# Four re-orderings in a four-layer convolution and scan kernel: gathers, tail units, the switch to layer 3, and half of T2

## The chip, the cores and the metric

The kernel runs on one NeuronCore of a Trainium2 chip. The metric is the device time of one execution in microseconds (us). TensorE is called PE, VectorE DVE, ScalarE ACT, GpSimd POOL and SyncE SP.

## The reference

The input x is a float32 image of 1024 channels and 64 x 64 positions. Four layers follow one another, each with a group norm ahead of it (32 groups) and a residual sum:

```python
x = x + L0(gn(x))   # a layer norm, then a decaying cumulative sum over the channels
x = x + L1(gn(x))   # 1x1 convolution, 1024 -> 1024, and bias
x = x + L2(gn(x))   # see below
x = x + L3(gn(x))   # 1x1 convolution, 1024 -> 1024, and bias

# L2
xz = silu(in_proj_w @ x + in_proj_b)           # 3072 rows: x_ssm, res, gate
x_ssm, res, gate = split(xz, 3)
xf = silu(conv1d(x_ssm, width 3, per channel)) # over the 4096 tokens
dt, B, C = dbc_w @ xf + dbc_b                  # 2 heads, 8 states
perm = argsort(score of a Mobius map)          # an order of the tokens for each head
# in that order: h = exp(dt*A)*h + dt*B*x ; y = C.h + D*x ; then back to the old order
y = y * silu(gate) + res
out = silu(out_proj_w @ y + out_proj_b)
```

## The kernel before, in words

Work runs in this order, one stage behind the other on PE: layer 0 (to about 385 us), layer 1 (to 620), the first third of layer 2's in_proj with its convolution over tokens (to 1075), a short tail of that stage (to 1127), the scan (to 1662), gate and out_proj (to 2375), layer 3 (to the end).

Image tiles are 128 channels by 512 positions (FB = 512), in pairs of position blocks (NP = 4 pairs); KH = 4 channel tiles make half the channels. The 1024 x 1024 products are made with a fast matrix scheme (Strassen and Winograd). In layer 1 and for the thirds WX and WR of in_proj it has one level: `multiply` (matmul at L832) makes seven products for each half of the output, with the operands b21, b11, b22 and the differences t2, t3, t1, t4, which `b_sets` prepares (L780 to L809): t1 = b12 - b11, t2 = b22 - t1, t3 = t2 - b11, t4 = b21 - t2, with `comb` at L790. It is a generator, so a caller advances it a step at a time; t1 is made on DVE and in most calls t2, t3, t4 on POOL. One such product is eight matmuls of 128 x 512, handed out as two "units" of about four, and `next_units(upto)` gives one more unit while fewer than `upto` were given.

For the gate, out_proj and layer 3 the scheme has two levels: `two_steps` runs jobs (gate and out for each pair, then "last" for layer 3), each with 7 outer products P1 to P7 of 7 inner products of eight 128 x 256 matmuls (L1670). A job takes 49 slots; `plan` hangs every other step (normalise, differences, additions, silu, statistics, loads) on a slot, and the loop at L1680 walks through the slots in order and writes each slot's product and then its steps into the queues. Odd slots belong to the outer product one step behind (L1682). The last out job has ORDER_C and ends with P7 and P4; the first job of layer 3 has ORDER_D and begins with P1 and P5. A name such as P4P5 is outer P4, inner P5. `next_norm` (L1479) puts the group norm of layer 3 on slots of the last out job: `begin` loads an ACT table set that holds Ln and Exp (L1485) and starts, each `go_on` takes one step (the matmuls gn_pg at L198 and gn_pv at L207, with DVE's gn_d between, L201 to L203), and `end` finishes (gn_v at L215, Ln and Exp at L168 and L169, scale and bias at L171 to L218). `fill` (L1438) applies the norm on ACT to make b11. Outputs of the out job pass an ACT silu (L1602), a DVE addition (L1604) and DVE statistics (L1477).

The engines' queues for these stages are written out by hand: inside `manual_schedule` the order of the Python calls is the order on DVE, PE, POOL and ACT. The loads that SP issues wait for their buffers.

The tail (L1239) follows the last convolution outputs (`follow`, `follow_on`) with a unit of WR between, up to six units; then `finish(NP - 1)` makes the last tokens' rows: silu of `end` (L1141), end_pt (L1143), end_dbc (L1151), softplus with Exp and Ln (L1162 to L1174), and DMAs of the rows into tok_d (L1186, L1188).

The scan goes through 74 chunks (NK). For chunk k: `gather` (POOL, L1266) brings 128 rows of tok_d into a tile "g"; `step_sums` (ACT, ds, L1274), `turn_rows` (PE, pr, L1280 and L1281), `spread_decay` (DVE), `cross` (PE, pg, L1302), `weigh` (DVE, G, L1310 to L1315), `apply` (PE, py, L1319, and ACT's copy y, L1324), `scatter` (POOL, L1328) into y_d. WR's units fill PE in between; their first parts go from PSUM into tiles "rg" (`put2b`, L1011 to L1014), and later parts are added there (L1018). POOL also sums weights for the later stages (s, L461 to L481). The loop at L1342 and on gathers four chunks ahead; PE gets eleven units ahead of chunk 0.

Of the kernel before, what the change touches and what calls it, by code (L numbers as in the profile page):

```python
# [9 lines left out]
F32 = mybir.dt.float32  # L10
# [8 lines left out]
P = 128  # L19
# [71 lines left out]
def tile_net(ctx: ExitStack, tc: tile.TileContext, x, par_d, cst_d, w_d, w2_d, dbcw_d, out):  # L91
# [141 lines left out]
        nc.sync.dma_start(tok_d[HEADS * N :, :], rows)  # L233


    lines = [const.tile([HEADS * NT, 2, P], F32, name=f"lines{i}") for i in range(2)]
    turned_ = [const.tile([P, 2, HEADS * NT], F32, name=f"turned{i}") for i in range(2)]
    swap = [const.tile([P, 2, P // 2], F32, name=f"swap{i}") for i in range(2)]
    order_i = const.tile([HEADS * NT, P], I32, name="order_i")
    nc.gpsimd.iota(order_i, pattern=[[1, P]], base=0, channel_multiplier=P)  # L240

    def make_scores():
# [534 lines left out]
    def b_sets(B, make, first=False, eng=None):  # L777

        def plain(name, row, col, upto=KH):
            B.setdefault(name, [])  # L780
            for k in range(len(B[name]), upto):
                t = b_tile(name, k, B["name"])
                make(t, row * KH + k, col)
                B[name].append(t)

        def comb(name, one, two, ks, eng):
            if name not in B:
                B[name] = [b_tile(name, k, B["name"]) for k in range(KH)]
            for k in ks:
                eng.tensor_tensor(B[name][k], B[one][k], B[two][k], ALU.subtract)  # L790

        slow = nc.vector if first else eng or nc.gpsimd
        plain("b21", 1, 0)
        yield
        plain("b11", 0, 0)
        yield
        plain("b22", 1, 1)
        yield
        for upto in (2, KH):
            plain("t1", 0, 1, upto)  # L800
            comb("t1", "t1", "b11", range(upto - 2, upto), nc.vector)
            yield
        comb("t2", "b22", "t1", range(KH), slow)
        yield
        for name, one, two in (("t3", "t2", "b11"), ("t4", "b21", "t2")):
            for ks in ((0, 1), (2, 3)):
                comb(name, one, two, ks, eng or nc.gpsimd)
                yield
# [196 lines left out]

    rg_pool = tc.tile_pool(name="l2r", bufs=2)
    rg_pools = [rg_pool.__enter__()]
    part, silus = {}, []  # L1010

    def put2b(m, o, nb, ps):
        part[o, nb] = rg_pools[-1].tile([P, FB], F32, tag="rg", name=f"rg{o}_{nb}")
        nc.scalar.copy(part[o, nb], ps)  # L1014

    def add2b(m, o, nb, ps):
# [12 lines left out]
    with tc.tile_pool(name="l2a", bufs=2) as pa, tc.tile_pool(name="l2a2", bufs=1) as pa2, \  # L1029
# [161 lines left out]
        with tc.manual_schedule(engines={E_.DVE, E_.PE, E_.Pool, E_.Activation}):  # L1191
            nc.sync.dma_start(both[:, :, P:], dbcw_d)
            nc.gpsimd.tensor_copy(both[:, :, :P], ident.unsqueeze(1).to_broadcast([P, CT, P]))
            nc.gpsimd.memset(row, 0.0)
            ends, i, chain = iter(()), -1, None
            for half in run(EARLY + LATE, [WX], normed(norm2), put2a, add2a, before2,
                            last_eng=nc.vector, fine=True, tell=True, begun=begun):
                if len(norm2) < CT:
                    n = len(SECOND)
                    if chain is None:  # L1200
                        moments("gn2b", SECOND, range(2, 4), mv2)
                        chain = norm_steps("gn2b", mv2[:, 0, :n], mv2[:, 1, :n], n, finer=True)
                        turns = 0
                    turns += 1
                    if turns < 3:
                        next(chain), next(chain)
                    else:
                        columns(SECOND, finish_of(chain), norm2)
                if half:
                    if coming[0] == "take":  # L1210
                        sort_on(True, 0)
                    if due3:
                        turn(*due3.pop(0))
                elif half is False:
                    turned = bool(due3)
                    follow()
                    follow_on()
                if half is not None:
                    continue
                i += 1  # L1220
                if i > 14 and i % 14 == 4:
                    ends = finish(i // 14 - 1)
                next(ends, None)
                if coming[0] != "turn" or not turned:
                    sort_on(True, (0, 0, 0, 1, 3, 1, 0, 2, 0, 2, 3, 3, 0, 0)[i % 14])
            while coming[0] is not None:
                sort_on(True, 1)

            forget(EARLY)
            units = run([3, 2] + EARLY, [WR], normed(norm2), put2b, add2b, before2, fine=True, B=last_B[0])  # L1230
            total, first, given = NP * 2 * NG * 7, 11, 0

            def next_units(upto):
                nonlocal given
                if given < upto:
                    given += 1
                    next(units, None)

            while ready or due or due2 or due3:  # L1239
                follow()  # L1240
                next_units(6)
                follow_on()
                next_units(6)
                activate(len(silus))
            for _ in finish(NP - 1):
                pass

    with tc.tile_pool(name="l2r2", bufs=8) as prg, tc.tile_pool(name="l2g", bufs=5) as pgat, tc.tile_pool(name="l2b", bufs=2) as pb, tc.tile_pool(name="l2h", bufs=1) as ph, \
            tc.tile_pool(name="ps2b", bufs=1, space=PSUM) as psb:
        rg_pools.append(prg)
        G2 = [ph.tile([P, P], F32, name=f"G{i}") for i in range(2)]
        B2 = [(ph.tile([MW, P], F32, name=f"bts{i}"), ph.tile([MW, S, LC], F32, name=f"cd{i}"))
              for i in range(2)]
# [81 lines left out]
        with tc.manual_schedule(engines={E_.DVE, E_.PE, E_.Pool, E_.Activation}):  # L1339
            while given < first:  # L1340
                next_units(total)
            for k in range(4):  # L1342
                gather(k)
            step_sums(0)
            for k in range(-1, NK + 1):
                upto = first + (k + 2) * (total - first) // (NK + 2)
                turned = turn_rows(k + 1) if k + 1 < NK else None
                if k > 0:
                    weigh(k - 1, pgs.pop(k - 1))
                if turned is not None:  # L1350
                    spread_decay(k + 1, *turned)
                if k + 2 < NK:
                    step_sums(k + 2)
                next_units(upto)
                y = apply(k - 1) if k > 0 else None
                if 0 <= k < NK:
                    pgs[k] = cross(k)
                if k + 1 < NK:
                    nc.scalar.activation(decay_[k + 1], decay_[k + 1], AF.Exp)
                if y is not None:  # L1360
                    scatter(k - 1, y)
                if 3 < k + 4 < NK:
                    gather(k + 4)
                next_units(upto)
                if given // 2 % 14 != 12:
                    next(sums, None)
                if len(silus) > 3:
                    activate(4)
            while given < total:
                next_units(total)  # L1370
            next(units, None)
            while silus:
                activate(4, nc.gpsimd)
            for _ in sums:
                pass
# [25 lines left out]
    def two_steps(jobs, norm2):  # L1401
# [76 lines left out]

        def next_norm(s0):  # L1479

            for row, slot, after, last in ((0, 44, (3, 3, 4, 4), 4), (1, 56, (3, 3, 4, 4), 5)):
                steps = {}

                def begin(row=row, steps=steps):
# [13 lines left out]
        def plan(j):  # L1498
# [9 lines left out]

            if kind != "out":
                for name, row, col, slot, when in (  # L1510
                        (("b11", 0, 0, -7, -1), ("b12", 0, 1, -3, 2), ("b21", 1, 0, 3, 12), ("b22", 1, 1, 8, 14))
                        if order is ORDER_D else
                        (("b11", 0, 0, -25, -14), ("b12", 0, 1, -14, -3), ("b21", 1, 0, -10, -1), ("b22", 1, 1, 1, 8))):
                    on(slot, fetch, src_d, pair, row, col, (j, "x", name))
                    for k in range(KH):
                        on(when + (k // 2 if when in (-1, 12) and order is ORDER_D else k), fill, j, name, row, col, k)
                late = [(1, "t1", "b12", "b11"), (9, "t2", "b22", "t1"), (13, "t3", "t2", "b11"), (27, "t4", "b21", "t2")]
                ks = [range(KH)] * 4
                put_in = {2: 12}
                if order is ORDER_D:  # L1520
                    late = [(2, "t1", "b12", "b11"), (16, "t2", "b22", "t1"), (20, "t3", "t2", "b11"), (27, "t4", "b21", "t2")]
                    put_in = {0: -1, 1: 5, 2: 13, 3: 19, 4: 24}
            else:
                late = [(14, "t1", "b12", "b11"), (15, "t2", "b22", "t1"), (19, "t3", "t2", "b11"), (34, "t4", "b21", "t2")]
                ks = [(2, 3, 0, 1), (2, 3, 0, 1), range(KH), range(KH)]
# [151 lines left out]
        for j in range(len(jobs)):  # L1677
            plan(j)
        end = len(jobs) * JOB
        for slot in range(min(at), max(max(at), end + 6) + 1):  # L1680
            step, i = divmod(slot, 7)
            if i % 2 == 1:  # L1682
                step -= 1
            if 0 <= step < 7 * len(jobs):
# [111 lines left out]
```

## Time and profile before

| | |
|---|---|
| median of 3 runs | 2735.13 us (2734.6 to 2735.33) |
| profiled execution | 2736.82 us |
| its span | 2735.0 us |
| PE busy in the span | 2613.8 us |
| DVE, POOL, ACT busy | 1804.5, 1224.4, 1089.8 us |
| mean granted PE clock | 0.983 of full |

The span runs from the first to the last record of the profiled execution; 1.8 us of its time lie outside. A wait is written as the engine that waits, the tile and line it wants to work on, and the engine, tile and line that released it, followed by the total in us, how often, and the longest. In a timeline a line has the start in us, the duration, engine, line, operation, output and input; idle time ahead of it and its releaser stand in square brackets. DMA lines show the issue, not the landing. The granted clock comes in stretches[...].

### The profile page before, as it was taken

To read this page: it belongs to the slowest core of one execution; us is meant where nothing else is said; L and a number is where in the kernel's file an instruction comes from. 1 tells how busy PE (TensorE), PEld (TensorE's weight loads), DVE (VectorE), ACT (ScalarE), POOL (GpSimd) and SP (SyncE) were. 2 spreads that over 40 slices of the span, in tenths; PEclk is the share of its full clock that TensorE was granted. 3 is DMA by queue.
4 is the path that set the end of the run, shared out by engine and by line. 5 is a ranking of instruction groups with operands and counts; after the bars stand their busy time and mean duration, and the time that the engine had idled before them with its cause. 6 is when DMAs were issued, how large, how long until landed. Compare 5 with 4: busy or idle time off the path is not lost.

```text
span 2735.0 us, 30900 instructions
## 1 busy us (share of the span) xinstructions
PE 2613.8 (96%) x9594; PEld 1726.7 (63%) x9594; DVE 1804.5 (66%) x3793; ACT 1089.8 (40%) x1840; POOL 1224.4 (45%) x1103
## 2 busy tenths in 40 slices
PE   4778999999999999999999999999999999999999
PEld 3664444444555555544444447888888888788887
DVE  7996765555445565477777665567576676777777
ACT  4783110104655654475757554322233133221220
POOL 4154224421112002357475655556575565555544
PEclk9998999999999999999999999999999999999999
DMA  7345557645433434587767874879899898788896
GB/s 286 119 166 185 175 206 262 202 131 202 162 106 107 138 129 102 162 267 223 228 195 226 274 222 144 243 246 304 217 277 292 239 304 234 251 289 294 298 328 214
DMA packets 423448, 591.46 MB, mean 216 GB/s; under 512 B 149973, under 2 KB 211541, under 8 KB 420214
## 3 DMA queue, kind: packets, MB, share of 16 engines
q1 hardware_dynamic: 298934, 365.76, 41.9%
q10 hardware_dynamic: 91456, 136.33, 14.2%
q0 software_dynamic: 32896, 87.40, 12.5%
q8 instruction: 78, 1.28, 0.2%
q14 instruction: 84, 0.69, 0.1%
HBM read 432.02 MB, written 157.36 MB: 215 GB/s over the span
## 4 chain that ended last, share of the span: by engine, by line
PE 47%; DMA 4%; POOL 3%; issue 3%; DVE 2%; ACT 1%; SPq 0%; POOLq 0%; DVEq 0%; ACTq 0%
PE mm L832 8%; PE q_P6P L1670 5%; PE q_P5P L1670 5%; PE q_P7P L1670 5%; PE q_P2P L1670 5%; PE q_P4P L1670 5%; PE q_P3P L1670 5%; PE q_P1P L1670 5%; DMA y_d<-y,dst 2%; PE py L1319 1%; POOL s L461 1%; PE pg L1302 1%; POOL t L790 1%; DMA g<-tok_d,src 0%; PE pr L1280 0%
## 5 line engine op out<-in xcount | busy, mean ns | idle before, releaser
L832 PE MATMUL mm<-t,w 128*128 128x512 f32 x1536 | 685.2, 597 | 4.6 <-POOL t L790 4.0
L832 PE MATMUL mm<-b,w 128*128 128x512 f32 x1152 | 516.4, 599 | 4.0 <-ACT b L936 2.9
L832 PEld LDWEIGHTS mm<-t,w 128*128 128x128 f32 x1536 | 286.7, 191 | 332.0 <-issue 318.1
L832 PEld LDWEIGHTS mm<-b,w 128*128 128x128 f32 x1152 | 216.8, 192 | 255.1 <-issue 243.7
L1328 POOL DMA_INDIRECT y_d<-y,dst x74 | 73.7, 996 | 184.6 <-ACT y L1324 107.4
L1055 DVE SCALAR_TENSOR_TENSOR cvp<-xs,par,cvp 128x512 f32<-128x512 f32 x128 | 95.3, 754 | 77.9 <-ACT cvp L1052 75.7
L1639 ACT COPY qQ<-q_P5P 128x512 f32<-128x512 f32 x48 | 28.1, 585 | 290.4 <-PE q_P5P L1670 239.5
L1082 POOL TENSOR_TENSOR acc<-l2xt,acc 128x136 f32<-128x136 f32 x56 | 28.2, 504 | 236.9 <-ACT l2xt L1076 233.6
L461 POOL TENSOR_TENSOR s<-s 128x256 f32<-128x256 f32 (+3 forms) x120 | 130.2, 1092 | 7.9
L790 POOL TENSOR_TENSOR t<-b,t 128x512 f32<-128x512 f32 x72 | 92.9, 1318 | 72.2 <-DVE t L790 48.1
L1322 ACT COPY g<-py 8x512 f32<-8x512 f32 x146 | 83.8, 574 | 95.0 <-PE py L1319 92.0
L1106 DVE TENSOR_TENSOR xs<-mm,xs 128x512 f32<-128x512 f32 x64 | 41.8, 684 | 117.8 <-PE mm L832 117.8
L951 DVE SCALAR_TENSOR_TENSOR image<-mm,par,image 128x512 f32<-128x512 f32 x64 | 47.2, 747 | 104.4 <-PE mm L832 104.3
L1310 DVE TENSOR_TENSOR E<-E,pg 128x512 f32<-128x512 f32 x74 | 50.7, 685 | 76.0 <-PE pg L1302 66.2
L1074 PEld LDWEIGHTS l2pt<-both,cv 128*128 128x128 f32 x512 | 77.2, 191 | 35.6 <-issue 24.6
L1438 ACT ACTIVATE qb<-x_x_b,gn_bias,gn_r_r 128x512 f32<-128x512 f32 x64 | 48.9, 806 | 113.9 <-DVE qQ L1600 50.5
L1670 PE MATMUL q_P4P<-t_t,wq_P4P 128*128 128x256 f32 x384 | 93.9, 389 | 0.0
L936 ACT ACTIVATE b<-image,gnl_bias,gnl_r_r 128x512 f32<-128x512 f32 x48 | 37.2, 809 | 138.1 <-PE mm L832 111.5
L1670 PE MATMUL q_P5P<-t_t,wq_P5P 128*128 128x256 f32 x384 | 90.8, 379 | 0.0
L1670 PE MATMUL q_P1P<-t_b,wq_P1P 128*128 128x256 f32 x384 | 90.6, 379 | 0.1
L1670 PE MATMUL q_P6P<-t_t,wq_P6P 128*128 128x256 f32 x384 | 90.7, 379 | 0.0
L1670 PE MATMUL q_P7P<-t_t,wq_P7P 128*128 128x256 f32 x384 | 90.7, 379 | 0.0
(415 smaller groups left out, 5914.6 us busy)
## 6 DMA issues: line engine op xcount, KB each, us to landing
w<-s_d SPq DMA_DIRECT2D x96, 512.0 KB
w<-in_w_dram SPq DMA_DIRECT2D x72, 512.0 KB
x_x_b<-x_d ACTq DMA_DIRECT2D x28, 1024.0 KB
image<-x_d SPq DMA_DIRECT2D x12, 2048.0 KB
wq_P6P<-s_d SPq DMA_DIRECT2D x84, 256.0 KB
wq_P7P<-s_d SPq DMA_DIRECT2D x84, 256.0 KB
wq_P5P<-s_d SPq DMA_DIRECT2D x84, 256.0 KB
wq_P3P<-s_d SPq DMA_DIRECT2D x84, 256.0 KB
```

Of the source, the lines that this page charges most:

```text
L461: eng.tensor_tensor(out, a, b, ALU.subtract)
L790: eng.tensor_tensor(B[name][k], B[one][k], B[two][k], ALU.subtract)
L832: nc.tensor.matmul(to[o], w[:, k, o * P : (o + 1) * P], B[name][k], start=(fresh and k == 0), stop=(k == KH - 1), skip_group_check=True)
L951: nc.vector.scalar_tensor_tensor(part, ps, pcol(bias_name, o), part, ALU.add, ALU.add)
L1055: nc.vector.scalar_tensor_tensor(cv, xo[:, at + t : at + t + FB], pcol("dww", 3 * o + t), cv, ALU.mult, ALU.add)
L1074: nc.tensor.matmul(pt[:, q * NV : (q + 1) * NV], cv[:, (q0 + q) * P : (q0 + q + 1) * P], both[:, o, :], start=True, stop=True)
L1106: nc.vector.tensor_tensor(part, ps, part, ALU.add)
L1310: nc.vector.tensor_tensor(Ef, Ef, pg, ALU.mult)
L1322: nc.scalar.copy(rows[k + 1][h * LC : h * LC + S, :DH], py[h * LC : h * LC + S])
L1328: nc.gpsimd.indirect_dma_start(out=y_d[:, :], out_offset=bass.IndirectOffsetOnAxis(ap=dst_[:, k : k + 1], axis=0), in_=y[:, :], in_offset= ...
L1438: nc.scalar.activation(tile_of(j, name)[:, k], held[j, "x", name][:, k], AF.Identity, bias=bias, scale=scale)
L1670: nc.tensor.matmul(ps[:, o, :], w[:, k, o * P : (o + 1) * P], rhs[:, k, :], start=(new and o == 0 and k == 0), stop=(k == 1), skip_group_c ...
```

## The change

Four things are re-ordered; no arithmetic is added or dropped.

- Gathers: five are issued ahead of the loop and chunk k + 5's in step k; six tiles "g" in place of five. The tiles of the token sort (lines, turned, swap, order_i) move into a pool that is closed ahead of the scan.
- Tail: up to eight units in place of six, with four "rg" tiles in the first pool in place of two; then `put2b` goes round a ring of ten tiles, six of the new pool and four of the old.
- The switch to layer 3: the first six slots of its first job are walked through in another order (1, 3, 5, 0, 2, 4), so the last three odd products of P4 come in a row ahead of the first three of P1; the steps of the first norm sit one or two slots later, and so do the first fills, the fetch of b21 and the first inner differences.
- T2: the first two of the four subtractions of t2 are written right behind t1's last ones, in the step before.

```diff
@@ -233,10 +233,12 @@
         nc.sync.dma_start(tok_d[HEADS * N :, :], rows)
 
 
-    lines = [const.tile([HEADS * NT, 2, P], F32, name=f"lines{i}") for i in range(2)]
-    turned_ = [const.tile([P, 2, HEADS * NT], F32, name=f"turned{i}") for i in range(2)]
-    swap = [const.tile([P, 2, P // 2], F32, name=f"swap{i}") for i in range(2)]
-    order_i = const.tile([HEADS * NT, P], I32, name="order_i")
+    sort_pool = tc.tile_pool(name="sort", bufs=1, side="right")
+    sorts = sort_pool.__enter__()
+    lines = [sorts.tile([HEADS * NT, 2, P], F32, name=f"lines{i}") for i in range(2)]
+    turned_ = [sorts.tile([P, 2, HEADS * NT], F32, name=f"turned{i}") for i in range(2)]
+    swap = [sorts.tile([P, 2, P // 2], F32, name=f"swap{i}") for i in range(2)]
+    order_i = sorts.tile([HEADS * NT, P], I32, name="order_i")
     nc.gpsimd.iota(order_i, pattern=[[1, P]], base=0, channel_multiplier=P)
 
     def make_scores():
@@ -799,8 +801,10 @@
         for upto in (2, KH):
             plain("t1", 0, 1, upto)
             comb("t1", "t1", "b11", range(upto - 2, upto), nc.vector)
+            if upto == KH:
+                comb("t2", "b22", "t1", range(2), slow)
             yield
-        comb("t2", "b22", "t1", range(KH), slow)
+        comb("t2", "b22", "t1", range(2, KH), slow)
         yield
         for name, one, two in (("t3", "t2", "b11"), ("t4", "b21", "t2")):
             for ks in ((0, 1), (2, 3)):
@@ -1005,12 +1009,15 @@
 
 
 
-    rg_pool = tc.tile_pool(name="l2r", bufs=2)
+    rg_pool = tc.tile_pool(name="l2r", bufs=4)
     rg_pools = [rg_pool.__enter__()]
     part, silus = {}, []
 
     def put2b(m, o, nb, ps):
-        part[o, nb] = rg_pools[-1].tile([P, FB], F32, tag="rg", name=f"rg{o}_{nb}")
+
+        at = rg_pools.pop(0)
+        rg_pools.append(at)
+        part[o, nb] = at.tile([P, FB], F32, tag="rg", name=f"rg{o}_{nb}")
         nc.scalar.copy(part[o, nb], ps)
 
     def add2b(m, o, nb, ps):
@@ -1238,20 +1245,22 @@
 
             while ready or due or due2 or due3:
                 follow()
-                next_units(6)
+                next_units(8)
                 follow_on()
-                next_units(6)
+                next_units(8)
                 activate(len(silus))
             for _ in finish(NP - 1):
                 pass
 
-
-
-
-
-    with tc.tile_pool(name="l2r2", bufs=8) as prg, tc.tile_pool(name="l2g", bufs=5) as pgat, tc.tile_pool(name="l2b", bufs=2) as pb, tc.tile_pool(name="l2h", bufs=1) as ph, \
+    sort_pool.__exit__(None, None, None)
+
+
+
+
+
+    with tc.tile_pool(name="l2r2", bufs=6) as prg, tc.tile_pool(name="l2g", bufs=6) as pgat, tc.tile_pool(name="l2b", bufs=2) as pb, tc.tile_pool(name="l2h", bufs=1) as ph, \
             tc.tile_pool(name="ps2b", bufs=1, space=PSUM) as psb:
-        rg_pools.append(prg)
+        rg_pools[:] = [prg] * 6 + rg_pools * 4
         G2 = [ph.tile([P, P], F32, name=f"G{i}") for i in range(2)]
         B2 = [(ph.tile([MW, P], F32, name=f"bts{i}"), ph.tile([MW, S, LC], F32, name=f"cd{i}"))
               for i in range(2)]
@@ -1339,7 +1348,7 @@
         with tc.manual_schedule(engines={E_.DVE, E_.PE, E_.Pool, E_.Activation}):
             while given < first:
                 next_units(total)
-            for k in range(4):
+            for k in range(5):
                 gather(k)
             step_sums(0)
             for k in range(-1, NK + 1):
@@ -1359,8 +1368,8 @@
                     nc.scalar.activation(decay_[k + 1], decay_[k + 1], AF.Exp)
                 if y is not None:
                     scatter(k - 1, y)
-                if 3 < k + 4 < NK:
-                    gather(k + 4)
+                if 4 < k + 5 < NK:
+                    gather(k + 5)
                 next_units(upto)
                 if given // 2 % 14 != 12:
                     next(sums, None)
@@ -1478,7 +1487,7 @@
 
         def next_norm(s0):
 
-            for row, slot, after, last in ((0, 44, (3, 3, 4, 4), 4), (1, 56, (3, 3, 4, 4), 5)):
+            for row, slot, after, last in ((0, 44, (4, 4, 5, 5), 6), (1, 56, (3, 3, 4, 4), 5)):
                 steps = {}
 
                 def begin(row=row, steps=steps):
@@ -1508,18 +1517,18 @@
 
             if kind != "out":
                 for name, row, col, slot, when in (
-                        (("b11", 0, 0, -7, -1), ("b12", 0, 1, -3, 2), ("b21", 1, 0, 3, 12), ("b22", 1, 1, 8, 14))
+                        (("b11", 0, 0, -7, 1), ("b12", 0, 1, -3, 2), ("b21", 1, 0, 5, 12), ("b22", 1, 1, 8, 14))
                         if order is ORDER_D else
                         (("b11", 0, 0, -25, -14), ("b12", 0, 1, -14, -3), ("b21", 1, 0, -10, -1), ("b22", 1, 1, 1, 8))):
                     on(slot, fetch, src_d, pair, row, col, (j, "x", name))
                     for k in range(KH):
-                        on(when + (k // 2 if when in (-1, 12) and order is ORDER_D else k), fill, j, name, row, col, k)
+                        on(when + (k // 2 if when in (1, 12) and order is ORDER_D else k), fill, j, name, row, col, k)
                 late = [(1, "t1", "b12", "b11"), (9, "t2", "b22", "t1"), (13, "t3", "t2", "b11"), (27, "t4", "b21", "t2")]
                 ks = [range(KH)] * 4
                 put_in = {2: 12}
                 if order is ORDER_D:
                     late = [(2, "t1", "b12", "b11"), (16, "t2", "b22", "t1"), (20, "t3", "t2", "b11"), (27, "t4", "b21", "t2")]
-                    put_in = {0: -1, 1: 5, 2: 13, 3: 19, 4: 24}
+                    put_in = {0: 2, 1: 5, 2: 13, 3: 19, 4: 24}
             else:
                 late = [(14, "t1", "b12", "b11"), (15, "t2", "b22", "t1"), (19, "t3", "t2", "b11"), (34, "t4", "b21", "t2")]
                 ks = [(2, 3, 0, 1), (2, 3, 0, 1), range(KH), range(KH)]
@@ -1677,8 +1686,11 @@
         for j in range(len(jobs)):
             plan(j)
         end = len(jobs) * JOB
+
+        s3 = turning * JOB
+        instead = {s3 + i: s3 + p for i, p in enumerate((1, 3, 5, 0, 2, 4))}
         for slot in range(min(at), max(max(at), end + 6) + 1):
-            step, i = divmod(slot, 7)
+            step, i = divmod(instead.get(slot, slot), 7)
             if i % 2 == 1:
                 step -= 1
             if 0 <= step < 7 * len(jobs):
```

## The prediction, on record before the change was run

> **What bounds the kernel now.** I read busy shares first, then the list of waits of TensorE (PE), then busy time by stage, then the timeline at each wait that the change touches. The page and the list of waits say:
>
> ```profile
> span 2735.0 us, 30900 instructions
> PE 2613.8 (96%) x9594; PEld 1726.7 (63%) x9594; DVE 1804.5 (66%) x3793; ACT 1089.8 (40%) x1840; POOL 1224.4 (45%) x1103
> PE pr L1280 <- DMA g<-tok_d,src: 7.6, 5, 2.8
> PE q_P1P L1670 <- ACT qb L1438: 5.4, 3, 2.7
> PE l2pt L1074 <- ACT l2xt L1076: 4.1, 1, 4.1
> PE mm L832 <- POOL t L790: 4.0, 1, 4.0
> ```
>
> PE is the bound: 2735.0 - 2613.8 leaves 121 us idle, about 77 of it in the first 400 us, which the change doesn't touch. So an edit can win only a PE wait and the half-clock time after it. By stage (columns: busy time of PE, PEld, DVE, ACT, POOL, granted clock, DMA share, GB/s):
>
> ```profile
> 1080.00:1110.00 30.00, 25.88 (x89) 15.13 (x88) 9.71 (x21) 13.54 (x26) 2.36 (x5) 0.94 0.35 107
> 1110.00:1130.00 20.00, 20.00 (x66) 9.32 (x65) 4.53 (x21) 7.32 (x16) 6.97 (x12) 1.00 0.70 201
> 1550.00:1600.00 50.00, 42.94 (x106) 19.39 (x106) 28.30 (x63) 23.52 (x43) 27.05 (x29) 0.93 0.84 262
> 2360.00:2412.00 52.00, 43.49 (x173) 34.79 (x172) 35.84 (x71) 24.64 (x38) 16.41 (x13) 0.87 0.76 260
> ```
>
> Late in the scan 7.1 us are idle and (1 - 0.93) x 50 = 3.5 us go to the clock; at the start of layer 3 it is 8.5 idle and 0.13 x 52 = 6.8 of clock. The hand-over to the scan (1110 to 1130) loses nothing: remember that row.
>
> **What the Trainium skill says.** "TensorE: Matmul & The Clock Gate", Part 1, "What's actually happening": the clock halves after at least one idle window of about 3.4 us and comes back after a busy one. The trace agrees on the sizes: eight matmuls of 128x256 take 1.89 us, but 3.76 after the 3.00 us wait at 2368.44. An idle stretch of some 3 us or more thus costs about 1.7 us on top (half of one window). "ScalarE: Activation LUTs", "What ACT_TABLE_LOAD costs": 1283 ns and a drain of 1380 ns. The trace has 1.28 us and no drain behind it (the load at 2380.02 is followed by ACTIVATE at 2381.32), so I use 1.28. The same page, "Table sets", says Ln and Exp share one set that can be loaded once; before, one load at 2361.91 serves both. "DMA: Bandwidth & Descriptors", "Anatomy of one DMA", has about 2 us fixed plus bytes; the gathers here measure more, 4.2 us when the DMA queues are light (1122.36 to 1126.54) and 5.5 to 5.9 late in the scan, which I use.
>
> **Gathers five chunks ahead (L1342, L1362).** POOL late in the scan, with the scatter (L1328) ahead of each gather (L1266):
>
> ```profile
> 1577.45 1.00 POOL L1328 DMA_INDIRECT y_d<-y,dst  x1
> 1578.75 0.96 POOL L1266 DMA_INDIRECT g<-tok_d,src  x1 [0.30 <-issue]
> 1583.96 1.00 POOL L1328 DMA_INDIRECT y_d<-y,dst  x1 [4.25 <-DMA y_d<-y,dst]
> 1585.27 0.97 POOL L1266 DMA_INDIRECT g<-tok_d,src  x1 [0.30 <-issue]
> 1584.72 0.55 PE L1280 MATMUL pr<-cst,g 128*112 128x192 f32 x2 [2.58 <-DMA g<-tok_d,src]
> ```
>
> The gather issued at 1578.75 is chunk 65's, which PE wants 3.4 us later and gets after 5.9. The five waits are 0.59, 0.19, 2.81, 2.58 and 1.41 us. One chunk more of lead is worth a period, (1644.16 - 1127.15) / 73 = 7.1 us. Chunks 63 to 66 together owe 6.8 us, and 2 to 3.5 more once PE isn't slowed: chunk 66 would be wanted near 1583.3. Its gather now takes the place of 65's and lands near 1584.7, so 1.3 us may stay. Gain: 7.6 + 3.5 - 1.3, **10 us** (4 to 12.5: POOL may slip, or all goes). The fifth gather ahead of the loop costs POOL 1.3 us, hidden: PE waits for the first alone. The count of instructions stays. Six buffers for g let the gather run without waiting for an earlier chunk's readers. The ring of ten rg tiles: the copies into them wait for PE (ACT's rg for mm, 37.7 us in 22 waits), none of weight for a tile. 0 (-0.5 to +0.5). Moving the sort's tiles frees room and has no instruction of its own.
>
> **Eight units in the tail (next_units(8), four l2r tiles).** The built order has the whole t2 product (8 matmuls) and one of t3 ahead of end_pt (L1143), where before there were one of t2. Before:
>
> ```profile
> 1110.80 0.27 PE L1143 MATMUL end_pt<-cst,end 128*8 128x128 f32 x1
> 1112.43 1.28 ACT L1165 ACT_TABLE_LOAD   x1
> 1113.96 1.28 ACT L1172 ACT_TABLE_LOAD   x1
> ...
> 1122.36 1.08 POOL L1266 DMA_INDIRECT g<-tok_d,src  x1 [0.17 <-issue]
> 1126.54 0.35 ACT L1274 ACTIVATE ds<-cst,g 128x64 f32<-128x64 f32 x1 [2.04 <-DMA g<-tok_d,src]
> 1127.15 0.49 PE L1280 MATMUL pr<-cst,g 128*112 128x192 f32 x2
> ```
>
> This is one chain: end_pt, softplus with two table loads, the last rows to HBM, the memsets that wait for those rows to land, gather 0, pr0. It takes 15.7 us, and before 18 matmuls of 0.857 us = 15.4 us of PE work lie beside it, so PE waits for nothing. After: t2 from 1109.95, 8 x 0.857 to 1116.8; the two rg copies (L1014, 0.59 each) stand ahead of `end` on ACT, which in turn stands ahead of end_pt: 1116.85 + 0.59 + 0.21, end_pt near 1117.75 instead of 1110.80, 6.95 us later. pr0 stays behind the eleventh unit, and only 11 matmuls (9.4 us) are left beside the chain. Its end moves to 1126.55 + 6.95 = 1133.5, PE is done at 1127.2: 6.3 us idle, and 1.7 of clock: **+8 us** (0 if the rows get out earlier by a path that I don't see, 9.5 with two half-clock windows). The 4.1 us wait at 1087.62 keeps its order: ACT's l2xt copy stands behind the same rg copies. 0.
>
> **Last quarters in a row ahead of layer 3 (L1481, L1511, L1680).** Before:
>
> ```profile
> 2361.91 1.28 ACT L1485 ACT_TABLE_LOAD   x1
> 2368.44 0.59 PE L198 MATMUL gn_pg<-gn_mv,cst 128*128 128x4 f32 x2 [3.00 <-DVE gn_mv L181]
> 2372.45 0.43 PE L207 MATMUL gn_pv<-gn_d,cst 128*128 128x4 f32 x2
> 2375.61 3.78 PE L1670 MATMUL q_P1P<-qb,wq_P1P 128*128 128x256 f32 x8 [2.74 <-ACT qb L1438]
> ```
>
> Four P4 and three P1 products alternate and are done at 2390.08. In the new order P4P7, P4P5, P4P4, P4P3 come first, then P1P1, P1P2, P1P6: the four P4 products (4 x 1.73 = 6.9 us) are to cover the norm's chain, which needed 7.2 us from pg to P1P1. But the chain grows. On ACT two silus of Q (L1602) now stand around the norm's Ln and Exp, so the preload is lost and the built order has four more loads: silu, Ln's, Exp's, silu's again. On DVE, Q's add and statistics stand inside the norm. Step by step: mv ends 2368.4, pg follows; P4P7 is done at 2367.2, but P4P5 waits for DVE to empty its bank: 2370.2 to 2372.1; d after one more add (0.6) at 2372.4; pv 2372.5; P4P4, P4P3 to 2376.1. DVE: two adds for P4P5, Q's add and statistics (4 x 0.65), v at 2375.1. ACT: Ln 2375.4, load 1.28, Exp 2376.9, load 1.28, silu 0.7: 2378.9. DVE: Q's second add and statistics 2380.3, four small operations 2381.1. Two fills of 0.8: P1P1 near 2382. PE idles 2376.1 to 2382 and pays half a clock again; P1P1 3.5, P1P2 1.9 to 3.5, P1P6 1.8: all seven done 2389 to 2391, against 2390.08. **+0.5**. P4P3's result is on DVE ten us sooner, so of the three small waits behind (1.08, 0.68, 0.56) I take 1.0 as gone: **-0.5** in all. Bounds: -13 (all idle and clock of the switch) to +5 (half clock throughout and P5P1's inputs late). SP's weight loads follow the new order ten buffers ahead; b21's fetch moves two slots later and is used from slot 12 on: 0.
>
> **Half of T2 in another step (L803).** In layer 1 no POOL instruction lies between its old place and the new, so the 4.0 us wait for t (L790) stays: there t2 sits behind s (L470), which waits 27.4 us for its DMA. In the scan two t2 (2.5 us) move ahead of one scatter and gather, three times; the longer lead covers it. 0 (-6.4 with its clock, if the order helped, to +1).
>
> **Sum**, against the profiled execution (2736.82 us, span 2735.0 and 1.8 around it): -10 + 8 - 0.5 = -2.5, so 2734.3. That execution lies 1.7 us above the median of 2735.13: **2732.6**, rounded 2732.5. Its own range: gathers -12 to -7, tail +6 to +9.5, switch -3 to +4: 2727 to 2740.
>
> **The rivals.** (1) *The switch works as meant*: the loads hide, P1P1 finds its input as P4P3 ends; 10 of the 13 us go, to 2736.8 - 10 + 8 - 10 - 1.7 = 2723; with the tail covered too, 2715. For it: 6.9 us of products against a chain of 7.2. Against: four loads, and Q on DVE within the norm. (2) *The slow side: POOL paces the gathers*. At 1583.96 the scatter ahead of the gather waits 4.25 us for the scatter before it to land; when these chained scatters (6.5 us each, against a period of 7.1) and the sums set the pace, the extra lead is spent once and the waits return later in the scan. Then the gathers give 1 us and the rest stands: 2736.8 - 1 + 7.5 - 1.7 = 2741.6. It decides from a gather gain under 2 us. For it: 12 such waits, 41.2 us. Against: they stop after chunk 67, and the debt is about one period. (3) *The change doesn't do what it says*: T2's move leaves layer 1's order as it is; I have that in the forecast. If it did act, 2726.
>
> **Chances.** Forecast 0.43, rival 1 0.32, rival 2 0.22, rival 3's opposite 0.03. 0.2% is about what a measurement of this kernel can tell from no change: below 2729.7 or above 2740.6. Faster: rival 1 0.30, the forecast's low end 0.05, the last 0.02: 0.37. Slower: rival 2's 0.20 and 0.03 of the forecast: 0.23. Same 0.40. To leave out no more than 0.2: 2717 to 2744.
>
> **What would show it.** Gathers: the wait of pr for g (7.6 us) nearly gone, ACT's ds for g far below its 82.0 us. Tail: a new wait of 6 us at pr0 near 1127; without it that step is wrong. Switch: four more table loads near 2365 to 2380 and a wait of about 6 us at P1P1; if P1P1 follows P4P3 at once, rival 1 holds. T2: the 4.0 us wait at t remains. Waits for g after chunk 60 as before would mean rival 2.

## The result and the profile after

The changed kernel takes 2742.88 us in the median of 10 runs (2740.66 to 2744.64); the kernel before took 2735.23 us beside it. The ratio is 1.0027, with a 95% interval of 1.0017 to 1.0037: slower by 7.65 us, where 2.6 us faster was forecast. The profiled execution took 2742.01 us, its span is 2740.2 us. From the page, and from the list of waits of PE (waiting tile, releaser, total in us, times, longest):

```profile
span 2740.2 us, 30909 instructions
PE 2615.7 (95%) x9594; PEld 1730.0 (63%) x9594; DVE 1807.8 (66%) x3793; ACT 1093.3 (40%) x1843; POOL 1223.4 (45%) x1103
PE py L1328 <- DVE G L1324: 11.2, 9, 2.6
PE q_P1P L1679 <- ACT qb L1447: 7.2, 2, 5.0
PE pr L1289 <- ACT ds L1283: 4.9, 1, 4.9
PE l2pt L1081 <- ACT l2xt L1083: 4.9, 2, 4.1
PE mm L836 <- POOL t L792: 4.6, 1, 4.6
```

The waits of pr for a gather (7.6 us) are gone. Two things are new in and ahead of the scan: the 4.9 us wait at pr0, and the doubled wait of py for G, of which the list of before says:

```profile
PE py L1319 <- DVE G L1315: 5.6, 8, 1.2
```

The same by stage after (busy PE, PEld, DVE, ACT, POOL, then granted clock, DMA share, GB/s):

```profile
1080.00:1113.00 33.00, 28.12 (x94) 16.22 (x93) 9.69 (x21) 14.07 (x27) 2.83 (x6) 0.95 0.39 123
1113.00:1150.00 37.00, 32.11 (x92) 15.14 (x91) 13.95 (x41) 14.88 (x24) 7.45 (x12) 0.91 0.50 143
1200.00:1560.00 360.00, 349.00 (x937) 167.99 (x936) 258.81 (x551) 224.44 (x387) 218.16 (x219) 0.99 0.77 228
1560.00:1627.00 67.00, 66.75 (x181) 32.00 (x180) 48.52 (x107) 33.55 (x61) 39.85 (x40) 1.00 0.91 269
2360.00:2425.00 65.00, 56.55 (x238) 47.10 (x238) 47.83 (x86) 32.39 (x46) 27.01 (x20) 0.92 0.77 266
```

Late in the scan (fourth row) nothing is lost now; 7.1 us idle and 3.5 of clock were. The hand-over to the scan (second row) lost nothing and now loses 4.9 us idle and 0.09 x 37 = 3.3 of clock. The middle of the scan (third row) is what the prediction hadn't on its list: 11.0 us idle at a clock of 0.99, where before 6.5 us were idle at 1.00. Over 360 us two decimals are too coarse for the clock; short stretches around the three places at which py now waits longer give it. First the row of before, then the three places after:

```profile
1200.00:1560.00 360.00, 353.50 (x957) 168.93 (x956) 260.36 (x567) 226.08 (x389) 222.12 (x222) 1.00 0.79 233
1227.00:1238.00 11.00, 8.40 (x19) 4.34 (x20) 9.05 (x21) 3.57 (x7) 7.02 (x8) 0.84 0.69 198
1374.00:1390.00 16.00, 13.96 (x39) 6.61 (x38) 14.52 (x30) 6.43 (x14) 8.88 (x10) 1.00 0.36 102
1527.00:1537.00 10.00, 9.48 (x17) 4.64 (x18) 7.03 (x18) 3.11 (x7) 4.45 (x4) 0.66 0.81 257
```

The clock takes 0.16 x 11 + 0.34 x 10 = 5.2 us at the first and the third place and nothing at the second. So the middle of the scan loses 4.5 + 5.2 = 9.7 us more than before. The switch (fifth row of the table by stage) loses 8.5 idle and 5.2 of clock, against 8.5 and 6.8. The clock there differs as much between executions of the same code: in run 2 below, whose switch is that of before, 0.06 x 60 = 3.6 us of it went between 2360 and 2420.

**The tail**, in the timeline after:

```profile
1117.75 0.27 PE L1150 MATMUL end_pt<-cst,end 128*8 128x128 f32 x1
1127.24 0.35 POOL L1268 MEMSET G<- 128x128 f32 x2 [16.06 <-DMA tok_d<-row]
1128.99 1.08 POOL L1275 DMA_INDIRECT g<-tok_d,src  x1 [0.18 <-issue]
1132.75 0.35 ACT L1283 ACTIVATE ds<-cst,g 128x64 f32<-128x64 f32 x1 [7.31 <-DMA g<-tok_d,src]
1133.14 0.95 PE L1289 MATMUL pr<-cst,g 128*112 128x192 f32 x2 [4.89 <-ACT ds L1283]
```

The chain of before is here with every link, 6.95 us later at end_pt (1117.75 against 1110.80). POOL's bracket shows what held the memsets: the rows of tok_d had to land.

**The switch**, from the timelines of ACT and PE after:

```profile
2374.73 1.28 ACT L1611 ACT_TABLE_LOAD   x1 [4.49 <-DVE stats L1486]
2377.34 1.28 ACT L168 ACT_TABLE_LOAD   x1
2383.01 1.28 ACT L169 ACT_TABLE_LOAD   x1
2384.52 1.28 ACT L1611 ACT_TABLE_LOAD   x1
2377.22 2.82 PE L1679 MATMUL q_P4P<-t_t,wq_P4P 128*128 128x256 f32 x8 [1.35 <-DVE qV L1656]
2389.53 6.56 PE L1679 MATMUL q_P1P<-qb,wq_P1P 128*128 128x256 f32 x16 [4.96 <-ACT qb L1447]
```

The four loads around the silus of Q, one of the last out job's output blocks, are there (three more than before in sum), P4P5 waits for its bank, and P1P1 waits 5 us for its fill. The two idle stretches of before (3.00 and 2.74 us) have become 1.26, 1.35 and 4.96.

**The middle of the scan**, DVE and PE at one of the three places before, then DVE, POOL and PE after:

```profile
1362.86 1.28 DVE L790 TENSOR_TENSOR t<-t,b 128x512 f32<-128x512 f32 x2
1366.45 1.10 PE L1319 MATMUL py<-g,G 128*128 128x512 f32 x2 [0.26 <-DVE G L1315]
...
1373.90 3.08 DVE L792 TENSOR_TENSOR t<-t,b 128x512 f32<-128x512 f32 x2
1373.33 2.50 POOL L792 TENSOR_TENSOR t<-b,t 128x512 f32<-128x512 f32 x2
1379.27 1.10 PE L1328 MATMUL py<-g,G 128*128 128x512 f32 x2 [2.04 <-DVE G L1324]
```

DVE's second pair of t1 subtractions takes 3.08 us, and took 1.28 before, when nothing lay beside it. Beside it now lie POOL's two early t2 subtractions, which the change put there. G is made by the next DVE instructions, so it comes 1.8 us late, and PE waits 2.04 us where it waited 0.26.

### The profile page after: what moved, and what is told of

It is laid out like the page before. It is cut to its first block, busy times and chain, and to the rows that moved or that the text cites. A ratio compares the mean times of both kernels' runs of the same rounds, so it can differ in the third digit from the quotient of the medians.

```text
span 2740.2 us, 30909 instructions
## 1 busy us (share of the span) xinstructions
PE 2615.7 (95%) x9594; PEld 1730.0 (63%) x9594; DVE 1807.8 (66%) x3793; ACT 1093.3 (40%) x1843; POOL 1223.4 (45%) x1103
## 3 DMA queue, kind: packets, MB, share of 16 engines
q8 instruction: 78, 1.28, 0.2%
## 4 chain that ended last, share of the span: by engine, by line
PE 52%; DVE 3%; DMA 1%; issue 1%; ACT 1%; POOL 0%; SPq 0%; DVEq 0%; POOLq 0%; ACTq 0%
PE mm L836 10%; PE q_P1P L1679 5%; PE q_P5P L1679 5%; PE q_P3P L1679 5%; PE q_P2P L1679 5%; PE q_P6P L1679 5%; PE q_P7P L1679 5%; PE q_P4P L1679 5%; PE py L1328 2%; PE pg L1311 2%; PE pr L1289 1%; DMA wq_P6P<-s_d 1%; DVE pg L1321 0%; DVE rg L1025 0%; PE pr L1290 0%
## 5 line engine op out<-in xcount | busy, mean ns | idle before, releaser
L1679 PE MATMUL q_P2P<-t_b,wq_P2P 128*128 128x256 f32 x384 | 90.7, 379 | 0.0
```

The source lines that it names most:

```text
L1679: nc.tensor.matmul(ps[:, o, :], w[:, k, o * P : (o + 1) * P], rhs[:, k, :], start=(new and o == 0 and k == 0), stop=(k == 1), skip_group_c ...
```

## The experiments

Theory A (the expectations call it the shared port): the t2 half costs what it costs since two engines' subtractions with both inputs in SBUF lie side by side and POOL holds DVE up. Rivals: B, the longer gather lead or the other units shift the scan so that DVE is late by itself; C, the place in POOL's queue ahead of a scatter and a gather. Each time is a median, and each difference from before is taken against the kernel before as timed beside that run (2734.5 to 2735.5 us). Times of one kernel spread by some 2 to 8 us, so a difference of under 4 us between two runs decides nothing.

**1. The change without the early t2**

```diff
-            if upto == KH:
-                comb("t2", "b22", "t1", range(2), slow)
             yield
-        comb("t2", "b22", "t1", range(2, KH), slow)
+        comb("t2", "b22", "t1", range(KH), slow)
```

> The changed kernel with t2 made in one step again, all else as changed. Theory A (shared port: GpSimd's two early t2 subtractions lie on VectorE's two t1 subtractions, which take 1.9 us each in place of 0.7, so that py waits for G): the second wait of each pair falls from 2.0 to 2.6 us back to 0.3 to 1.2 us, the scan loses some 9 us less, about 2734 us, level with before. Theory B (the longer gather lead or the units given in the tail shift the scan's work so that VectorE comes late by itself): the waits for G stay near 11 us in sum and the time stays near 2743.

2733.46 us, ratio 0.9992 (0.9984 to 1.0000): 9.4 us less than the changed kernel. The waits for G are 5.3 us in sum; the place shown above:

```profile
1371.15 1.28 DVE L792 TENSOR_TENSOR t<-t,b 128x512 f32<-128x512 f32 x2
```

Theory B falls: gather lead and units are the same here. A is what is left of the two.

**2. The kernel before with the early t2 alone** (the two added lines and the third of the diff of the change).

> The kernel before with nothing but the two early t2 subtractions. Theory A: py's waits for G go from 5.6 to about 11 us in sum with half-clock time behind them, about 2744 us (+9). Theory B: as before, 2735.

2743.00 us, ratio 1.0034 (1.0021 to 1.0048); its profiled execution, with a span of 2737.3 us, is the fastest of its five. The waits for G are 8.8 us, not 11: one of the three places escaped. The waits for gathers fell from 7.6 to 4.6 us in the same execution, so this trace doesn't account for the 7.5 us of the median; what it shows is how the places differ. Its DVE and POOL, first the place that escaped, then the next:

```profile
1216.14 1.33 DVE L790 TENSOR_TENSOR t<-t,b 128x512 f32<-128x512 f32 x2
1217.68 2.49 POOL L790 TENSOR_TENSOR t<-b,t 128x512 f32<-128x512 f32 x2
...
1362.35 3.08 DVE L790 TENSOR_TENSOR t<-t,b 128x512 f32<-128x512 f32 x2
1361.78 2.50 POOL L790 TENSOR_TENSOR t<-b,t 128x512 f32<-128x512 f32 x2
```

At the first, POOL's gather ran late and t2 began 0.2 us after DVE had finished: no delay, and PE waited 0.32 us. At the next place t2 was under way when DVE came, and PE waited 2.04 us. The code and the queue are the same; only where the two engines overlapped was there a cost.

**3. The early t2 one step earlier still**, on the kernel before, so that DVE's second t1 pair has nothing of it beside it:

```diff
             comb("t1", "t1", "b11", range(upto - 2, upto), nc.vector)
+            if upto == 2:
+                comb("t2", "b22", "t1", range(2), slow)
             yield
-        comb("t2", "b22", "t1", range(KH), slow)
+        comb("t2", "b22", "t1", range(2, KH), slow)
```

> The kernel before with the first two t2 subtractions one step earlier still, right behind t1's first two, so that no t1 subtraction of VectorE lies beside them. Theory A (what hurts is the overlap of two engines' subtractions): VectorE's t1 pairs stay at 1.3 us, no new waits for G, 2735 within 2. If it is the place in GpSimd's queue ahead of a scatter and a gather that hurts (theory C): at least as slow as one step later, 2744 or more.

2730.15 us, ratio 0.9983 (0.9974 to 0.9991): not just harmless but a gain, which no theory had. C falls. The waits for gathers went from 7.6 to 3.0 us, which is 4.6 of the 5 us; why they fell is not shown (POOL may have the half of t2 behind it when the crowded steps come). Here DVE's subtraction began first at each place, since POOL's needs the t1 that DVE makes just ahead of it, and POOL gave way:

```profile
1206.92 1.28 DVE L790 TENSOR_TENSOR t<-t,b 128x512 f32<-128x512 f32 x2
1207.69 2.87 POOL L790 TENSOR_TENSOR t<-b,t 128x512 f32<-128x512 f32 x2 [2.86 <-DVE t L790]
```

DVE keeps its 1.28 us and POOL takes 2.87 in place of 2.50.

**4. One early subtraction in place of two**, on the kernel of run 2:

```diff
-                comb("t2", "b22", "t1", range(2), slow)
+                comb("t2", "b22", "t1", range(1), slow)
...
-        comb("t2", "b22", "t1", range(2, KH), slow)
+        comb("t2", "b22", "t1", range(1, KH), slow)
```

> The kernel before with one early t2 subtraction in place of two. Shared-port theory: GpSimd holds VectorE up for one subtraction (1.2 us) in place of two (2.0 to 2.3), so the t1 subtraction beside it takes 1.8 us in place of 2.5 to 2.8, the second waits of G are near 1.3 us and the time is 2738 to 2741. If VectorE merely shares bandwidth, its subtraction takes some 1.3 us.

2736.58 us, ratio 1.0005 (0.9996 to 1.0013). I expected 1.8 us for the delayed subtraction and 2738 at the least; both were too high. The pair takes:

```profile
1365.36 1.87 DVE L790 TENSOR_TENSOR t<-t,b 128x512 f32<-128x512 f32 x2
1364.80 1.27 POOL L790 TENSOR_TENSOR t<-b,t 128x512 f32<-128x512 f32 x1
```

POOL had 1364.80 + 1.27 - 1365.36 = 0.71 us to go when DVE's came. In the trace the first of DVE's two lasts 1.27 us there and 1.55 at the next place, where 0.99 us were to go: in both 0.56 us more than POOL's rest. With two POOL subtractions (run 2) it is 2.49 and 2.76 us, where the two together had 1361.78 + 2.50 - 1362.35 = 1.93 and, at the next place, 2.21 us to go: again 0.56 us more. So in all four cases DVE's subtraction, which takes 0.68 us alone, ended 0.56 us behind POOL's last one: it did next to nothing until POOL was through. The 1.27 us alone would also fit the 1.3 that the expectation gave for shared bandwidth. The four together don't: if DVE went at half its pace beside POOL, I estimate about 1.0 and 1.2 us for the rests of 0.71 and 0.99 (0.68 and half the rest), and no more than 2 x 0.68 = 1.36 for the longer ones. The delay fits in DVE's slack here, and the waits for G stay at 1.2 us and less.

**5. The change with six units in the tail**

```diff
-                next_units(8)
+                next_units(6)
```

(at both places.)

> The changed kernel with six units in the tail again. Tail theory (the chain from end_pt to pr0 lost 7 us of its cover): the wait of 4.9 us at pr0 and the 0.75 us wait in the tail go, 9 us less with the clock, about 2734. Rival (the wait comes from the fifth gather or the new pools): the wait stays, 2743.

2734.99 us, ratio 0.9998 (0.9990 to 1.0007): 7.9 us less than the changed kernel. There is no wait at pr0, and the second wait of l2pt in the tail (0.75 us in the change) is gone; the rest of the change is still in it.

**6. The tail part alone**, on the kernel before: next_units(8), four l2r tiles, six of the new pool and the ring.

> The kernel before with the tail part alone: up to eight units, the ring of ten rg tiles, nothing else. Tail theory: a wait of 5 us at pr0 and 0.75 us in the tail, with the half clock 9 us more, 2744. If the tail's loss needs the fifth gather or the new place of the sort's tiles: 2735.

2745.86 us, ratio 1.0040 (1.0026 to 1.0054):

```profile
1136.96 0.95 PE L1282 MATMUL pr<-cst,g 128*112 128x192 f32 x2 [5.42 <-ACT ds L1276]
```

The wait needs neither the fifth gather nor the moved tiles. It costs 10.8 us alone.

**7. More work beside the chain**: run 1 with 13 units ahead of chunk 0 in place of 11.

```diff
-            total, first, given = NP * 2 * NG * 7, 11, 0
+            total, first, given = NP * 2 * NG * 7, 13, 0
```

> The changed kernel with t2 in one step and 13 units ahead of the first chunk in place of 11, so that 8 more matmuls (6.9 us) lie beside the chain from end_pt to pr0. Tail theory (the wait at pr0 is lost cover, nothing else): the 5 us wait and its half clock go, some 7 us less than with 11 units (2733.5), about 2727. Rival (pr0 waits for something that also moves later with the units): the wait stays, 2733.

2725.98 us, ratio 0.9965 (0.9952 to 0.9979), 7.5 us less than run 1. PE goes through to pr0 without a wait:

```profile
1127.76 8.75 PE L834 MATMUL mm<-t,w 128*128 128x512 f32 x20
1136.34 0.49 PE L1287 MATMUL pr<-cst,g 128*112 128x192 f32 x2
```

So the tail's loss was lost cover: the chain is as long as before, and eight matmuls put back beside it pay for it.

**8. The gathers alone**, on the kernel before (five ahead, six tiles, the sort's pool).

> The kernel before with the gathers five chunks ahead, six g tiles and the sort's tiles in their own pool, nothing else. My step: pr's waits for g (7.6 us) go, with the half clock behind them 10 to 11 us less, about 2724.5. Rival (GpSimd sets the pace of the gathers and the waits come back later): 2732 to 2735.

2725.29 us, ratio 0.9965 (0.9952 to 0.9979): 9.2 us less. No wait of pr for g is left, and none has come back elsewhere in the scan: the waits for G are 5.5 us, as before.

**9. The switch alone**, on the kernel before.

> The kernel before with the new order at the switch to layer 3 only. My step: the products are in a row, but the norm's chain grows by three table loads and Q's silus, so 0.5 to 2 us less: 2733.5. Rival (the row of P4 products is worth most of the 13 us of idle and clock at the switch): 2725.

2734.52 us, ratio 0.9997 (0.9989 to 1.0005): no difference. The wait at P1P1 is 4.6 us.

**10. Gathers and switch together**

> Gathers and switch together, without the tail and t2 parts. If the parts add up: 2735 - 10.5 - 1.5 = 2723. If they don't (a part only helps where another one made room): the difference to the sum shows it.

2721.94 us, ratio 0.9957 (0.9943 to 0.9970). This is the lowest median of all: 12.6 us faster than before, 21 faster than the change as it was made. Runs 7, 8, 11 and 12 lie within some 4 us of it and can't be told from it. The switch is worth 3.4 us on top of run 8 and nothing in run 9, which is within the spread.

**11. The same, with Q's silus behind the norm**

```diff
-                done = (... ("Q", 1, 1, {2: 49, 3: 50, 0: 51, 1: 52}),
+                done = (... ("Q", 1, 1, {2: 51, 3: 52, 0: 53, 1: 54}),
```

> As gathers and switch together, with Q's four silus two slots later, behind the norm's Ln and Exp, so that one table load serves both again and Q's additions and statistics leave the norm's chain. If the table loads and Q inside the norm are what keeps the switch from gaining: the wait of 5 us at the first P1 product nearly goes with its half clock, 6 to 8 us less than gathers and switch, about 2716. If something else holds the fills (the image's load, the statistics): within 2 us of 2723.

2724.44 us, ratio 0.9963 (0.9950 to 0.9977): no gain. The edit did what it was to do, and the time didn't follow. PE:

```profile
2365.47 2.27 PE L1674 MATMUL q_P1P<-qb,wq_P1P 128*128 128x256 f32 x8 [0.56 <-ACT qb L1442]
2368.91 2.27 PE L1674 MATMUL q_P1P<-qb,wq_P1P 128*128 128x256 f32 x8 [1.18 <-ACT qb L1442]
...
2379.60 0.67 PE L1674 MATMUL q_P5P<-qb,wq_P5P 128*128 128x256 f32 x2 [1.36 <-issue]
2382.79 2.93 PE L1674 MATMUL q_P5P<-qb,wq_P5P 128*128 128x256 f32 x6 [2.52 <-DVE qb L1438]
```

The wait of 5.6 us at P1P1 fell to 0.56 and 1.18 us, and 3.9 us came up at P5P1, whose input DVE makes: Q's additions and statistics are now among V's and in front of it. So the table loads and Q inside the norm are not all that keeps the switch from gaining. That ACT's and DVE's work there has to be done before P5P1 in either order fits these waits; no run tests it.

**12. Run 10 with the t2 half of run 3**

> Gathers, switch and the t2 half in t1's first step together, without the tail part and without t2 in t1's second step. If the gains add up: 2735 - 12.6 (gathers and switch measured together) - 5 (t2 in t1's first step) = 2717.5. But the t2 half there mostly took waits for gathers away (7.6 to 3.0 us), and the longer lead takes the same waits: then nothing is added, about 2722.

2725.34 us, ratio 0.9966 (0.9952 to 0.9980). The first expectation (2717.5) fails. The second holds as far as this can tell: 3.4 us more than run 10 and than the 2722 expected, with intervals that overlap. No wait of pr for a gather is left in either run, so the t2 half had none to take away.

## Why the prediction was wrong

| step of the prediction | forecast | alone | taken out of the change |
|---|---|---|---|
| gathers | -10 | -9.2 (run 8) | |
| tail | +8 | +10.8 (run 6) | 7.9 (run 5) |
| switch | -0.5 | 0.0 (run 9); -3.4 on top of the gathers | |
| half of T2 | 0 | +7.5 (run 2) | 9.4 (run 1) |

The parts alone add up to -9.2 + 10.8 + 0.0 + 7.5 = +9.1 us, near the measured +7.65. The forecast was -2.5, so it is some 10 us off; the half of T2 is 9.4 of them (run 1).

*Half of T2* is the step that failed: "two t2 (2.5 us) move ahead of one scatter and gather, three times; the longer lead covers it. 0 (-6.4 with its clock, if the order helped, to +1)". It walked POOL's queue, found what stands behind the moved instructions, and covered that. What it didn't do is look at what DVE does at that time. The Trainium skill, "SBUF — State Buffer", "Who interferes with whom", says that a VectorE instruction with two SBUF inputs contends with a GpSimd instruction that reads SBUF, that the ports the two share are an exclusive lock, and that the order of issue decides which of them blocks. The runs agree as far as a trace can show it (runs 2, 3 and 4: a delay of 1.8 to 2.1 us beside two POOL subtractions, 0.6 to 0.9 beside one, none where DVE came first), with one addition: DVE waited for both of POOL's subtractions, not only for the one under way when it came. The trace of before had a hint:

```profile
1214.58 2.25 DVE L790 TENSOR_TENSOR t<-t,b 128x512 f32<-128x512 f32 x2
1214.41 0.74 POOL L470 TENSOR_TENSOR s<-s 128x256 f32<-128x256 f32 x1
1215.22 3.01 POOL L461 TENSOR_TENSOR s<-s 128x256 f32<-128x256 f32 x3
1219.15 1.10 PE L1319 MATMUL py<-g,G 128*128 128x512 f32 x2 [1.23 <-DVE G L1315]
```

A t1 pair beside POOL's s sums took 2.25 us in place of 1.28, and PE's wait of 1.23 us followed from it. The same lines bound the addition. DVE's pair was over at 1216.83, while POOL's sums ran on to 1218.23, and the last three of them took 3.01 us against 2.22 in run 2 (at 1220.93), where no t1 subtraction lay beside them. So here each engine let the other in between two instructions. Only the two t2 subtractions were waited out as a pair, in all five overlaps (three in the change, two in run 2); what makes that difference is not shown.

A delay of 1.8 us on DVE became some 10 us in the profiled execution, 9.4 by run 1: three places with 1.4, 1.8 and 2.1 us more of waiting, and 5.2 us of half clock behind the first and the third. The prediction charged half a clock to an idle stretch of some 3 us or more. In these traces it also followed shorter ones, here of 2.61 and 2.35 us but not of 2.04, and before the change one of 1.41 us (at 1592.12) but not one of 2.58 (at 1584.72). So the length of one wait doesn't tell whether the clock falls, and waits of under 3 us can't be taken as free of it. That T2's move leaves layer 1 as it is held: the wait there is 4.6 us.

*Gathers*: right, in place and size. Rival 2 (POOL sets the pace) falls with run 8.

*Tail*: right in its mechanism; in the change it costs 7.9 us (run 5), alone 10.8 (run 6), which is above the range of +6 to +9.5. In the profile of the change end_pt comes 6.95 us later, to the hundredth. The wait is 4.9 us in place of 6.3, since gather 0 was used 3.8 us after its issue, not 4.2, the rest of the chain was 0.3 us shorter, and PE's work was done at 1128.25, not 1127.2 (1118.54 and 9.71 us of it). The clock takes 3.3 in place of 1.7, the end of the range that it gave with two half-clock windows. A shorter wait and more of clock made up for each other, so that the sum of 8 came out closer than its terms.

*Switch*: right as a sum, and in the order of its waits. Rival 1 (the row of P4 products covers the norm) falls with run 9. The wait at P1P1 was put at 5.9 and is 5.0; net loads are three more, not four, since one of the four stood there before.

*T2 against the rest*: the time ended on the slow side by a mechanism that none of the rivals named. That rival 2's 2741.6 us lies near the measured time is chance.

## What to carry to other kernels

When an instruction moves in POOL's queue, write down what DVE runs in the same microseconds; if both are subtractions or additions with both inputs in SBUF, the one that comes second stands at least until the other engine's instruction is over, here even until a second one was, and what hangs on it comes late. A chain of small steps ahead of a loop is free as long as enough TensorE work is queued beside it: count that work (here 18 matmuls against 15.7 us) before moving any of it ahead of the chain's start. Changes that bundle several re-orderings are best run part by part: here two parts were worth -12.6 us and the other two cost more than that.

## What was not expected of the hardware

That a blocked DVE instruction can wait for a second POOL instruction too: two POOL subtractions cost it 1.8 to 2.1 us, one cost 0.6 to 0.9 us, and the same two cost it nothing where DVE began first. It isn't always so: between POOL's s sums DVE got in after one. And the cost in time wasn't in proportion: two early subtractions made 7.5 us, one made 1.5 us, which is within the spread.
